# A convolution, FFT-mixer and FFN block on one core: the mixer rewritten as a real DFT with mirror pairs

## The chip, the cores and the metric

One core of a Trainium2 chip runs the whole program. The metric is the device time of one execution in microseconds (us). The kernel before takes 9553.09 us in the three runs given with it (9535.19 to 9569.67). TensorE (PE) does matrix products, VectorE (DVE) and ScalarE (ACT) do elementwise work, GpSimd (POOL) is nearly idle, SyncE (SP) issues the transfers. A trace also records the clock that TensorE was granted: 1.0 is full speed, and here only 1.0 and 0.5 occur, so that a mean of 0.83 means one third of the time at half speed.

## The reference, cut to what matters

Input x is (32, 96, 56, 56) in fp32. Three layers follow one another.

```python
# 1. inverted-residual convolution, 96 -> 576 -> 96 channels, depthwise 3x3 between, + x
# 2. t: 3136 tokens of 96 channels per image
#    h = relu(bn(layer_norm(t) @ w1.T))              # 192 channels
#    X = fft(h, axis=tokens, norm='ortho')
#    xr = relu(X.real * rd - X.imag * id + rb)
#    xi = relu(X.imag * rd + X.real * id + ib)
#    y = ifft(xr + 1j * xi).real                     # along tokens
#    t = t + bn(y @ w2.T)                            # back to 96 channels
# 3. t = t + ffn(layer_norm(t)), operands quantised to fp8, sums to fp16
```

The transform has 3136 = 56 x 56 points and is done in two stages of 56 by matrix products, with twiddle factors between.

## The kernel before

Four streams of small jobs are interleaved by a schedule in units of one image: the convolution (a strip of 14 rows at a time, four strips an image), the projection with the first DFT stage, the spectrum (second stage, rectifier, first inverse stage), and the inverse with the FFN. The generators are "skewed": when a new job enters a stream, every job already in that stream advances by one stage.

The mixer before, with cuts marked:

```python
def project(img, s, g0):                  # tokens doubled: rows 0-55 real, 56-111 imaginary copy
    for q in range(g):                    # g = 4, 4, 4, 2 of the strip's 14 rows
        nc.tensor.matmul(pv[0:SK, q, 0:HA], lhsT=lnx[:, g0 + q, :, :]..., rhs=watt, ...)   # L457
    nc.vector.scalar_tensor_tensor(z, pv, 0.0, ri, ALU.max, ALU.mult)                       # L465
    yield
    for j in range(g // 2):
        nc.tensor.matmul(ps[0:SK, j, 0:2*HA], lhsT=wa, rhs=z[:, 2*j:2*j+2, :], ...)         # L476
    # ... ACT evacuates to ya, transfer to DRAM
def spectrum(img, kg):                    # 14 jobs of 4 columns an image
    # ... load yb
    for q in range(4):
        nc.tensor.matmul(pv[0:SK, q, 0:HA], lhsT=wb[:, 4*kg+q, :], rhs=yb[:, q, :], ...)    # L518
    evacuate(v, pv, relu=True)
    yield
    for j in range(2):
        nc.tensor.matmul(ps[0:SK, j, 0:2*HA], lhsT=wc, rhs=v[:, 2*j:2*j+2, :], ...)         # L526
    # ... evacuate to gc, transfer to DRAM
    inverted[img] = inverted.get(img, 0) + 4
def spectrum_jobs(img):
    for kg in range(S // 4):
        yield lambda: projected.get(img) == S, spectrum(img, kg)
def mix_ffn(img, ng):                     # 8 jobs an image
    nc.sync.dma_start(out=gd, in_=...)
    yield
    ps = psum()
    for q in range(NG):
        for c in range(2):
            nc.tensor.matmul(ps[0:C, c, ...], lhsT=gd[:, q, C*c:C*(c+1)], rhs=wd[:, NG*ng+q, :], ...)  # L550
    evacuate(y, ps)
    yield
    # w2a on y (L562), add to the tokens, layer norm (L245, L257, L274), FFN ...
def ffn_jobs(img):
    for ng in range(S // NG):
        yield lambda: inverted.get(img) == S, mix_ffn(img, ng)     # the gate
    # ... as many empty steps
```

The convolution, which the change does not touch, runs eight of nine taps of 512 channels on DVE, the ninth on ACT, and the remaining 64 channels on PE:

```python
for dr, dc in TAPS:                       # 9
    if (dr, dc) == (0, 0):
        nc.scalar.activation(dst, src, AF.Copy, scale=w)
    else:
        nc.vector.scalar_tensor_tensor(dst, src, w, dst, ALU.mult, ALU.add)    # L386
```

## Time and profile before

| | before |
|---|---|
| span of the profiled run | 9559 us |
| PE busy, mean granted clock | 8315 us, 0.835 |
| DVE busy | 6353 us |
| ACT busy | 3542 us |
| moved by transfers | 712 MB |
| period of one image in the steady state | 288 us |

The period is read from the instruction that finishes a strip's tokens (128 of them): the first starts at 120.1 us, the last at 9266.6 us, so (9266.6 - 120.1) / 127 x 4 = 288 us. Busy shares are unions of intervals; in a row of a group the busy time is followed by the mean duration of one instruction. A matmul's duration is modelled; its cost in a dense stream is the distance from one start to the next. The prediction shows the lines themselves.

### The profile page before, as it was taken

What the parts mean: (1) busy time and instruction counts of PE and PEld (TensorE: products, weight loads), DVE (VectorE), ACT (ScalarE), POOL (GpSimd) and SP (SyncE); (2) the same over time, 40 slices, a digit from 0 to 9 for tenths busy, and PEclk for the clock granted to TensorE, in tenths of its full rate; (3) what the DMA queues carried; (4) which work ended last, traced back from release to release, by engine and by line L of the source; (5) the groups of instructions that cost most, each with busy time, mean ns of one, the idle gap of its engine ahead of it and who ended that gap; (6) DMA issues with size and microseconds to landing.
All of it is one profiled execution on the core that took longest, in us unless ns stands there. A gap on an engine that the chain in (4) does not pass through costs nothing.

```text
span 9559.2 us, 100499 instructions
## 1 busy us (share of the span) xinstructions
PE 8315.1 (87%) x39424; PEld 5424.0 (57%) x39424; DVE 6353.1 (66%) x10129; ACT 3542.0 (37%) x4744; POOL 13.2 (0%) x72
## 2 busy tenths in 40 slices
PE   5888889888898888898888988888988888888888
PEld 2555556555565555555555655555655556555566
DVE  6766676666766667766677666676666776666753
ACT  2333343333433334433334333344333343333432
POOL 0000000000000000000000000000000000000000
PEclk8988798887987888888889878888888888888986
DMA  1222222222222222222222222222222222222222
GB/s 44 67 76 72 77 73 77 71 73 78 77 72 76 70 77 79 68 83 72 73 80 73 77 76 73 75 79 68 80 74 70 82 65 82 72 75 79 76 85 81
DMA packets 582785, 711.58 MB, mean 74 GB/s; under 512 B 35484, under 2 KB 476520, under 8 KB 582088
## 3 DMA queue, kind: packets, MB, share of 16 engines
q1 hardware_dynamic: 582314, 705.17, 25.6%
q8 instruction: 312, 5.11, 0.2%
q14 instruction: 159, 1.30, 0.0%
HBM read 358.22 MB, written 346.82 MB: 74 GB/s over the span
## 4 chain that ended last, share of the span: by engine, by line
PE 64%; DVE 22%; ACT 7%; DMA 3%; issue 3%; SPq 0%; ACTq 0%; DVEq 0%
DVE acc L386 16%; PE ps L550 10%; PE ps L562 6%; PE ps L274 5%; PE ps L358 5%; PE ps L526 5%; PE po L402 5%; PE ps L245 5%; PE ps L335 4%; PE ps L257 4%; PE ps L476 4%; PE ps L518 4%; PE ps L457 3%; ACT acc L389 2%; DVE z L465 2%
## 5 line engine op out<-in xcount | busy, mean ns | idle before, releaser
L386 DVE SCALAR_TENSOR_TENSOR acc<-hs,wdw,acc 128x770 f32<-128x770 f32 (+3 forms) x4096 | 4072.0, 1007 | 124.8 <-ACT acc L384 86.5
L402 PE MATMUL po<-acc,w2T 128*96 128x392 f32 x2048 | 941.0, 573 | 430.7 <-ACT acc L389 430.7
L550 PEld LDWEIGHTS ps<-wd,gd 112*96 112x96 f32 x7168 | 1046.0, 247 | 341.5 <-issue 307.5
L550 PE MATMUL ps<-wd,gd 112*96 112x56 f32 x7168 | 1031.5, 331 | 183.0 <-DMA gd<-gdr 183.0
L235 DVE COPY gc<-ps 112x768 f32<-112x768 f32 x417 | 397.5, 953 | 879.6 <-PE ps L526 879.6
L358 PE MATMUL ps<-xs,w1T 96*128 96x448 f32 x2048 | 861.7, 548 | 8.8 <-ACT ya L480 7.9
L389 ACT ACTIVATE acc<-acc,sbd 128x784 f32<-128x784 f32 x512 | 531.7, 1039 | 720.7 <-DVE acc L386 718.5
L402 PEld LDWEIGHTS po<-acc,w2T 128*96 128x96 f32 x2048 | 355.9, 187 | 779.0 <-ACT acc L389 563.5
L366 ACT ACTIVATE hs<-ps,sb 128x896 f32<-128x896 f32 x512 | 558.6, 1091 | 562.0 <-PE ps L358 561.9
L476 PE MATMUL ps<-z,wa 112*112 112x384 f32 x1792 | 743.2, 535 | 6.2 <-DVE z L465 6.2
L457 PE MATMUL ps<-watt,lnx 97*112 97x192 f32 x3584 | 721.0, 344 | 0.0
L245 PE MATMUL ps<-t,mean_w 96*96 96x392 f32 x1024 | 565.3, 664 | 161.3 <-ACT acc L389 97.0
L457 PEld LDWEIGHTS ps<-watt,lnx 97*112 97x112 f32 x3584 | 629.7, 188 | 132.8 <-issue 35.3
L526 PE MATMUL ps<-v,wc 112*112 112x384 f32 x1792 | 692.5, 510 | 5.7 <-ACT v L231 5.5
L518 PEld LDWEIGHTS ps<-yb,wb 114*112 114x112 f32 x3584 | 594.8, 177 | 180.1 <-issue 54.8
L518 PE MATMUL ps<-yb,wb 114*112 114x192 f32 x3584 | 673.8, 328 | 2.6 <-DMA yb<-ydr 2.6
L480 ACT ACTIVATE ya<-ps 112x768 f32<-112x768 f32 (+1 forms) x512 | 370.6, 724 | 741.2 <-PE ps L476 741.2
L562 PE MATMUL ps<-y,w2a 96*96 96x392 f32 x1024 | 599.0, 728 | 33.8 <-DVE y L235 32.9
L465 DVE SCALAR_TENSOR_TENSOR z<-ps,ri 112x768 f32<-112x768 f32 (+1 forms) x512 | 436.8, 853 | 234.3 <-PE ps L457 231.3
L358 PEld LDWEIGHTS ps<-xs,w1T 96*128 96x128 f32 x2048 | 372.3, 190 | 339.4 <-issue 266.1
L526 PEld LDWEIGHTS ps<-v,wc 112*112 112x112 f32 x1792 | 327.4, 187 | 292.4 <-issue 127.7
L235 DVE COPY y<-ps 96x784 f32<-96x784 f32 x128 | 124.2, 971 | 553.2 <-PE ps L550 553.2
(142 smaller groups left out, 8533.8 us busy)
## 6 DMA issues: line engine op xcount, KB each, us to landing
yb<-ydr SPq DMA_DIRECT2D x448, 336.0 KB, 3.3
gdr<-gc SPq DMA_DIRECT2D x448, 336.0 KB, 3.9
gd<-gdr SPq DMA_DIRECT2D x256, 588.0 KB, 4.4
ydr<-ya SPq DMA_DIRECT2D x384, 336.0 KB, 2.7
xs<-in_x_dram SPq DMA_DIRECT2D x128, 336.0 KB, 3.2
out_dram<-t SPq DMA_DIRECT2D x256, 147.0 KB, 1.9
ydr<-ya SPq DMA_DIRECT2D x128, 168.0 KB
wb<-in_wb_dram SPq DMA_DIRECT2D x1, 2793.0 KB
```

The lines of the kernel that those rows point to most:

```text
L245: nc.tensor.matmul(ps[0:C, j, 0:per], lhsT=mean_w, rhs=t[:, j * per : (j + 1) * per], start=True, stop=True)
L358: nc.tensor.matmul(ps[:, j, 0:448], lhsT=w1T[:, 128 * k : 128 * (k + 1)], rhs=xt[:, 8 * j : 8 * j + 8, :], start=True, stop=True,)
L386: nc.vector.scalar_tensor_tensor(dst, src, w, dst, ALU.mult, ALU.add)
L389: nc.scalar.activation(a2, a2, AF.Relu, bias=sbd[:, 1, k : k + 1], scale=sbd[:, 0, k : k + 1])
L402: nc.tensor.matmul(po[img, s][0:C, j, 0:NB2], lhsT=w2T[:, k, :], rhs=a2[:, NB2 * j : NB2 * (j + 1)], start=False, stop=(k == NK - 1),)
L457: nc.tensor.matmul(pv[0:SK, q, 0:HA], lhsT=lnx[:, g0 + q, :, :].rearrange("p a c -> p (a c)"), rhs=watt, start=True, stop=True,)
L465: nc.vector.scalar_tensor_tensor(z[:, 0:g, :], pv[0:SK, 0:g, 0:HA], 0.0, ri.unsqueeze(1).to_broadcast([SK, g, HA]), ALU.max, ALU.mult,)
L476: nc.tensor.matmul(ps[0:SK, j, 0 : 2 * HA], lhsT=wa, rhs=z[:, 2 * j : 2 * j + 2, :], start=True, stop=True)
L518: nc.tensor.matmul(pv[0:SK, q, 0:HA], lhsT=wb[:, 4 * kg + q, :], rhs=yb[:, q, :], start=True, stop=True)
L526: nc.tensor.matmul(ps[0:SK, j, 0 : 2 * HA], lhsT=wc, rhs=v[:, 2 * j : 2 * j + 2, :], start=True, stop=True)
L550: nc.tensor.matmul(ps[0:C, c, q * S : (q + 1) * S], lhsT=gd[:, q, C * c : C * (c + 1)], rhs=wd[:, NG * ng + q, :], start=True, stop=True,)
L562: nc.tensor.matmul(ps[0:C, 0, 0:NW], lhsT=w2a[:, c, :], rhs=y[:, c, :], start=(c == 0), stop=(c == 1))
```

## The change

The input of the transform is real, so of the 56 first-stage outputs only 29 are independent, and the outputs of the second stage pair up with their mirror images. The change uses this: (1) the first norm is folded into centred weights and a scale per token, so that tokens are no longer doubled; (2) 28 slots replace 56 columns in the spectrum, and the data, not the constants, are the stationary operand; (3) the rectifier works on both members of a mirror pair at once, in ten elementwise instructions instead of one; (4) the second projection w2a stands ahead of the inverse, so that the inverse works on 96 channels instead of 192. The core of the diff:

```diff
-            nc.tensor.matmul(pv[0:SK, q, 0:HA], lhsT=lnx[...], rhs=watt, ...)
+            nc.tensor.matmul(pv[0:SK, q, 0:HA], lhsT=ts[:, SK*k:SK*(k+1)], rhs=watt, ...)   # 7, not 14, a strip
+            nc.vector.scalar_tensor_tensor(z[:, q, :], pv[0:SK, q, 0:HA], fac[...], nsh, ALU.mult, ALU.max)
 ...
-    for q in range(4): matmul(..., lhsT=wb[:, 4*kg+q, :], rhs=yb[:, q, :])
-    evacuate(v, ..., relu=True)
+    for c in range(2):                                    # channel halves
+        for q in range(n): matmul(..., lhsT=yb[:, q, C*c:C*(c+1)], rhs=wb[:, s0+q, :])      # 114 columns
+        nc.scalar.activation(p, a, AF.Identity, bias=rb, scale=r)
+        nc.scalar.activation(m, b, AF.Abs, scale=i)
+        nc.scalar.activation(z[:, :, 0:NF], a, AF.Relu, bias=rb2, scale=r2)
+        nc.vector.tensor_add(m, m, p)
+        nc.vector.tensor_max(z[:, :, 0:NF], z[:, :, 0:NF], m)
+        nc.scalar.activation(u, a, AF.Identity, bias=ib, scale=i)
+        nc.vector.scalar_tensor_tensor(t, b, nr, u, ALU.mult, ALU.add)
+        nc.scalar.activation(t, t, AF.Relu)
+        nc.vector.scalar_tensor_tensor(u, b, r, u, ALU.mult, ALU.add)
+        nc.vector.scalar_tensor_tensor(z[:, :, NF:NF2], u, 0.0, t, ALU.max, ALU.subtract)
+        yield
+    for q in range(n):
+        for c in range(2): matmul(..., lhsT=zs[:, c, q, :], rhs=w2a[:, c, :])                # to frequencies
 ...
 def spectrum_jobs(img):
-    for kg in range(S // 4):
-        yield lambda: projected.get(img) == S, spectrum(img, kg)
+    for s0 in range(0, P2, Q):                            # 4 jobs of 8 slots, each with 3 empty steps
+        yield lambda: projected.get(img) == P2, spectrum(img, s0)
+        for _ in range(3):
+            yield True, iter(())
 ...  # mix_ffn
-    for q in range(NG):
-        for c in range(2): matmul(..., lhsT=gd[:, q, C*c:C*(c+1)], rhs=wd[:, NG*ng+q, :])    # 14, 56 columns
-    evacuate(y, ...); yield; w2a on y
+    for q in range(g): matmul(..., lhsT=gd[:, q, :], rhs=wd[:, t0+q, :])                     # 3 or 4, 112 columns
```

## The prediction

> **What bounds the kernel now.** I read the page's busy shares and slices first, then the timeline of TensorE (to get real matmul rates), then stretches of one image's period, because shares are averages over unlike stages.
>
> The page's header, busy shares and slice rows:
>
> ```profile
> span 9559.2 us, 100499 instructions
> ...
> PE 8315.1 (87%) x39424; PEld 5424.0 (57%) x39424; DVE 6353.1 (66%) x10129; ACT 3542.0 (37%) x4744; POOL 13.2 (0%) x72
> ...
> PE   5888889888898888898888988888988888888888
> ...
> DVE  6766676666766667766677666676666776666753
> ...
> PEclk8988798887987888888889878888888888888986
> DMA  1222222222222222222222222222222222222222
> ```
>
> PE is busy 87% but its granted clock is only 0.7 to 0.9; DMA is at two tenths and cannot be the bound. Matmul durations are modelled, so I take rates from start to start in the PE timeline (start, us, ..., count), in a stretch at full clock:
>
> ```profile
> 3016.74 2.51 PE L550 MATMUL ps<-wd,gd 112*96 112x56 f32 x28
> 3019.09 1.56 PE L274 MATMUL ps<-ident,ra 98*96 98x98 f32 x16
> ...
> 3051.32 0.92 PE L274 MATMUL ps<-ident,rf 98*96 98x98 f32 x8
> 3052.08 0.81 PE L257 MATMUL ps<-mean_w,sqf 96*98 96x1 f32 x8
> ...
> 3055.00 1.45 PE L526 MATMUL ps<-v,wc 112*112 112x384 f32 x4
> 3056.29 1.47 PE L518 MATMUL ps<-yb,wb 114*112 114x192 f32 x8
> 3057.59 0.67 PE L589 MATMUL ps<-h,w2q 128*96 128x392 fp8e5 x3
> ```
>
> 384 columns: 1.29/4 = 322 ns a record; 192 columns: 1.30/8 = 163 ns; 98 columns: 0.76/8 = 95 ns; 56 columns behind 96 weight columns (L550): 2.35/28 = 84 ns. An fp32 matmul of the program leaves two records (L526: 14 groups x 2 x 32 images = 896 matmuls, 1792 records). So wide matmuls cost 0.84 ns a column and record, thin ones never less than their weight load. Applying such rates to all counts gives **about 6790 us of PE work at full clock**, over the page's mean clock 0.835 some 8130 us, 85% of the span: PE is the bound on average.
>
> Stretches of one image (columns: length, then busy us of PE, PEld, DVE, ACT, POOL, then clock, DMA share, GB/s) show that this is a mixture:
>
> ```profile
> 5072.00:5096.00 24.00, 23.80 (x121) 15.84 (x120) 23.21 (x46) 14.50 (x23) 0.00 (x0) 1.00 0.33 95
> ...
> 5192.00:5216.00 24.00, 16.34 (x45) 7.89 (x44) 23.71 (x26) 9.51 (x10) 0.00 (x0) 0.83 0.12 36
> ...
> 5240.00:5264.00 24.00, 17.97 (x76) 11.42 (x75) 12.50 (x13) 7.42 (x10) 0.00 (x0) 0.89 0.60 173
> 5264.00:5288.00 24.00, 22.94 (x94) 16.80 (x94) 5.46 (x12) 1.97 (x4) 0.00 (x0) 0.50 0.27 76
> 5288.00:5312.00 24.00, 23.92 (x120) 18.75 (x120) 7.23 (x24) 4.58 (x8) 0.00 (x0) 0.54 0.19 51
> ...
> 5264.00:5324.00 60.00, 58.85 (x311) 42.02 (x310) 14.89 (x38) 11.35 (x18) 0.00 (x0) 0.62 0.24 63
> 5324.00:5552.00 228.00, 193.68 (x908) 121.96 (x906) 182.71 (x277) 99.19 (x131) 0.30 (x2) 0.91 0.27 79
> ```
>
> The period is 288 us (13.9 strips of tokens end per 1000 us, four make an image). Some 228 us of it are a mixed stage in which DVE is 80% and PE 85% busy, with DVE full at times (23.71 of 24). The other 60 us are a **burst**: the inverse transform of an image is gated on all its spectrum, and at the gate six steps of mix-and-FFN come with no convolution between them. PE first waits 5.2 us for the data just written to DRAM, then runs L550, L562 and the norms at clock 0.50, with DVE idle.
>
> **What the Trainium skill says.** (1) "TensorE: Matmul & The Clock Gate", section on LDWEIGHTS: a load takes columns / 1.2 ns. The trace agrees: 98 columns give 82 ns, and the L257 records (98 weight columns, 1 moving) start (3052.75 - 3052.08)/8 = 84 ns apart, the next row of that timeline starting at 3052.75. (2) The same page, Part 1: the clock halves after an idle window and returns after about 3.4 us of activity. The halving agrees (0.50 after the 5.2 us wait); the return does not: PE is 99% busy for 48 us and stays near 0.50. I read this as thin, load-bound matmuls not counting as activity; that is a guess. (3) "ScalarE: Activation LUTs", section What ACT_TABLE_LOAD costs: 186 ns + 0.833 ns an element, each pointer operand about 93 ns more. Here a PSUM copy of 768 takes 804 ns (the page gives 826), a scaled copy of 784 takes 946 (932). (4) "VectorE: DVE Perf Modes", Why PSUM operands drop a tier: fp32 with a PSUM operand is one element a cycle at most. Agrees: 112x384 takes 555, 112x768 takes 952 ns, so 1.03 ns an element.
>
> **The change part by part.** All sums over 32 images; PE at full clock.
>
> *PE removed* (records x ns): wd L550 7168 x 84 = 602; w2a L562 1024 x 330 = 338; wb L518 and projection L457 3584 x 163 = 584 each; wc L526 and wa L476 1792 x 322 = 577 each; the first norm's three matmul groups (half of L245, the a-parts of L257 and L274) 169 + 168 + 195 = 532. Sum 3794.
>
> *PE added*: thin matmuls (96 to 114 columns, weights as wide) I put at 105 ns, from the 95 ns of the 98/96 shape. Norm 1 as centred product, 7 a strip, 1792 records = 188; forward wb 2 x 28 x 32 x 2 = 3584 records = 376; second projection the same 376; wd 28 x 32 x 2 = 1792 records = 188. Projection without doubled tokens, 1792 x 163 = 292; wa 28 x 192 columns an image at 2 x 0.84 ns = 289; wc on 28 x 96 columns = 144. Sum 1853. **PE falls by 1941, from 6790 to 4850**, 152 us an image; at 0.83 that is 183.
>
> *DVE removed* (summed durations of rows): evacuations v, gc, y (30 + 398 + 124), z 437, lnx 236, cena 123, small norm work 127: 1475. *Added*: z is now 896 ops of 192 with a pointer scalar, 200 + 210 = 410 ns each, 367 us (the L564 row, 392 from PSUM with pointer, is 620 ns, hence 210 fixed); small norm work 127 again; the rectifier, five ops on 8 x 57 = 456 elements: 624, 624, 686, 686, 627 = 3.25 us, on 4 x 57 2.06 us; an image has 6 of the first and 2 of the second, 23.6 us, 755 in all. Sum 1250. Rows overlap by some 7% (their sum is 6.8 ms, the page's busy 6.35), so DVE goes from 6353 to **about 6140, 192 us an image**. The convolution, 4072 in L386 alone, is untouched.
>
> *ACT*: removed v, gc, y, ya, sqa = 947. Added 896 squares of 96 with a sum (260 ns) 233; ya 206; rectifier 722 + 630 + 722 + 722 + 580 = 3.4 us (2.4 for the small block), 803; g and gc 185. Sum 1427. From 3542 to about 4000: not a bound.
>
> *DMA*: per image 112 x 56 x 192 x 4 B four times becomes half of it twice and a quarter twice: less than half. It was hidden; only the wait at the gate remains, and a smaller constant load at the start (10 to 15 us of the 57 us first wait).
>
> *Moved*: DVE is now the larger load in the mixed stage. An image's burst needs about half the matmul work, since L562 and its evacuation are gone and wd has 14 or fewer thin records for each old 28 + 28: six steps of about 11 us at full clock, 22 to 25 at half. So an image takes: DVE outside the burst 192 - 8 = 184 us at 91% saturation (in the stretches above where PE is not full, DVE reached 91 to 99%) = 202; the stall at the gate 8 to 10; the burst 25: **236 us instead of 288**. First strip at 120 becomes 107; tail after the last strip 293 becomes about 185 (it is mixer and FFN of two images at low clock). Total 107 + 31.75 x 236 + 185 = 7785; I shade it to 7700, as the burst might nearly fill with conv work once PE is free.
>
> **Rivals.** *PE sets it still*: if PE, idling more and running thin matmuls, is held at 0.6, its 152 us become 253 an image and the span 8300 or more. For: clock 0.50 in the burst with PE busy. Against: in the mixed stage the same thin norms ran at 0.91 to 1.00. *The rectifier's ping-pong*: ACT and DVE hand t and u back and forth, each in strict order, with one of three PSUM buffers held some 6 us, 8 times an image; if all of it stood on the path, 40 us an image, 8900 us. Against: other streams lie between, and PSUM allocations fall from about 156 to 104 an image. *DVE saturates fully*: 6140/0.93 = 6600, if the gate vanished too. For: 99% in one stretch. Against: the gate's rule is unchanged (the last stage of the last block still waits for the next image's first step).
>
> **Range and chances.** 82% DVE saturation with a 35 us burst gives 31.75 x 269 + 292 = 8830, 96% with 20 us 31.75 x 220 + 292 = 7280. The first needs several losses at once. I take 7200 to 8200. All rivals but extreme ones beat 9553, so a gain over 2% is nearly sure.
>
> **What would show it.** DVE busy 6.0 to 6.3 ms and about 80% of the span; PE work well under it; wb and second projection near 105 ns start to start; ACT near 4.0 ms; one burst an image of 20 to 30 us at clock near 0.5. It would be wrong if the clock in the mixed stage falls below 0.75, if ACT or DVE show long waits on sp, sm, st, su, or if the thin matmuls take 150 ns or more at full clock.

## More of the kernel before

The schedule's entries give the start and the length of a stream in images:

```python
[skewed(every(conv_jobs)),     ..., 0.0,  1.0, 0],
[skewed(project_jobs()),       ..., 0.3,  1.0, 0],
[skewed(every(spectrum_jobs)), ..., 1.45, 0.8, 0],
[skewed(every(ffn_jobs)),      ..., 2.2,  0.9, 0],
```

## The result, and the profile after

The changed kernel takes 7801.02 us (7785.22 to 7816.11, 4 runs), the kernel before 9544.14 in the same rounds: a ratio of 0.8172, 95% interval 0.8143 to 0.8201. Ratios here are the mean time of one kernel's runs over that of the other's of the same rounds, so not quite the ratio of the medians quoted. Executions over 1.5% slower than the fastest of the same kernel are left out of the means.

The page after, header, busy shares and slices:

```profile
span 7814.3 us, 81935 instructions
...
PE 6311.2 (81%) x29442; PEld 3988.3 (51%) x29442; DVE 5984.6 (77%) x10834; ACT 3932.8 (50%) x7245; POOL 9.5 (0%) x70
...
PE   3788888888888878888888888888888888888887
...
DVE  4878778778787787787787877877777877778864
...
PEclk9877887778877788877788787788787888877876
DMA  1111111111111111111111111111111111111111
```

PE lost 2004 us of busy time and DVE 369, ACT gained 391. PE's clock did not rise with the lighter load, it fell from 0.835 to 0.802. A useful sum is span = DVE busy + DVE idle: before 6353 + 3206, after 5985 + 1830. Of the 1745 us between the two profiled spans, 1376 are idle time of DVE and 369 its work. The chain of work that ended last, by engine, before and after, still lies mostly on PE:

```profile
PE 64%; DVE 22%; ACT 7%; DMA 3%; issue 3%; SPq 0%; ACTq 0%; DVEq 0%
```

```profile
PE 60%; DVE 20%; ACT 13%; DMA 3%; issue 2%; SPq 1%; another core or an unknown queue 0%; DVEq 0%; ACTq 0%
```

Groups of the DVE and ACT lists by shape (busy us, mean ns of one, then idle before and who ended it):

```profile
L520 DVE SCALAR_TENSOR_TENSOR z<-ps,ra,nsh 112x192 f32<-112x192 f32 x896 | 355.4, 409 | 152.7 <-PE ps L515 150.6
L596 DVE SCALAR_TENSOR_TENSOR su<-ps,ric,su 96x456 f32<-96x456 f32 x192 | 131.4, 684 | 2.2
L591 DVE TENSOR_TENSOR sm<-sm,sp 96x456 f32<-96x456 f32 x192 | 120.0, 625 | 134.6 <-ACT sm L589 134.6
...
L497 ACT ACTIVATION_READ_ACCUMULATOR sqa<-ps 112x1 f32 x896 | 175.3, 196 | 0.0
```

The new DVE ops cost what was predicted (409, 684 and 625 ns against 410, 686 and 624). The last row was not foreseen: each of the 896 squares with a sum is followed by a second ACT instruction of 196 ns that reads the sum out.

TensorE's timeline around the gate of one image (start, us, group; in brackets idle before it and its cause):

```profile
4095.01 1.56 PE L448 MATMUL po<-acc,w2T 128*96 128x392 f32 x4 [1.51 <-ACT acc L435]
4100.93 1.78 PE L648 MATMUL ps<-wd,gd 112*96 112x112 f32 x8 [4.37 <-DMA gd<-gdr]
...
4106.27 1.91 PE L448 MATMUL po<-acc,w2T 128*96 128x392 f32 x4
...
4124.05 1.73 PE L573 MATMUL ps<-wb,yb 113*96 113x114 f32 x16
4125.71 1.72 PE L350 MATMUL ps<-xs,w1T 96*64 96x448 f32 x4
```

The wait for gd, the spectrum read back from DRAM for the inverse, is still there (4.37 us), and convolution matmuls (L448, L350) now stand between the mix-and-FFN steps. The 16 thin records of L573 take (4125.71 - 4124.05) / 16 = 104 ns each at full clock.

Two views of stretches of the changed kernel, 24 us each around that gate, then one whole period (length, busy us of PE, PEld, DVE, ACT, POOL, clock, DMA share, GB/s):

```profile
4072.00:4096.00 24.00, 19.48 (x57) 11.01 (x56) 23.23 (x35) 12.21 (x28) 0.00 (x0) 0.69 0.17 49
4096.00:4120.00 24.00, 15.64 (x67) 10.79 (x66) 17.44 (x33) 5.75 (x9) 0.14 (x1) 0.73 0.40 94
4120.00:4144.00 24.00, 21.25 (x128) 14.42 (x130) 11.77 (x32) 13.20 (x23) 0.00 (x0) 0.77 0.16 38
...
4108.00:4168.00 60.00, 53.59 (x333) 36.65 (x331) 38.33 (x92) 32.53 (x62) 0.00 (x0) 0.86 0.16 43
4168.00:4342.00 174.00, 137.13 (x583) 83.80 (x583) 145.93 (x244) 89.45 (x163) 0.28 (x2) 0.81 0.15 42
```

A period is 234 us ((7589.2 - 160.3) / 127 x 4), of which DVE is busy 184. Of its 50 us of idle time, 22 lie in the 60 us behind the gate and 28 in the other 174, where it is 84% busy. Just before the gate DVE is nearly full (23.23 of 24) while PE is 19.48 of 24 us busy at clock 0.69. That PE's pauses cost it its clock there is argued; b_warm, below, shows it for one other pause.

The starts and ends: the first strip is finished at 160 us, 40 later than before; after the last strip 225 us are left, against 293 before.

### The profile page after: what moved, and what is told of

The parts are those of the page before. It is cut to its first block, busy times and chain, and to the rows that moved or that the text cites. A ratio compares the mean times of both kernels' runs of the same rounds, so it can differ in the third digit from the quotient of the medians.

```text
span 7814.3 us, 81935 instructions
## 1 busy us (share of the span) xinstructions
PE 6311.2 (81%) x29442; PEld 3988.3 (51%) x29442; DVE 5984.6 (77%) x10834; ACT 3932.8 (50%) x7245; POOL 9.5 (0%) x70
## 4 chain that ended last, share of the span: by engine, by line
PE 60%; DVE 20%; ACT 13%; DMA 3%; issue 2%; SPq 1%; another core or an unknown queue 0%; DVEq 0%; ACTq 0%
DVE acc L432 13%; PE po L448 9%; PE ps L404 6%; PE ps L602 6%; PE ps L381 5%; PE ps L515 4%; PE ps L291 4%; PE ps L320 3%; PE ps L648 3%; PE ps L528 3%; PE ps L487 3%; PE ps L573 3%; PE ps L303 3%; PE ps L350 3%; DMA gd<-gdr 2%
## 5 line engine op out<-in xcount | busy, mean ns | idle before, releaser
L432 DVE SCALAR_TENSOR_TENSOR acc<-hs,wdw,acc 128x770 f32<-128x770 f32 (+2 forms) x4096 | 4035.3, 1005 | 73.9 <-ACT acc L430 51.4
L448 PE MATMUL po<-acc,w2T 128*96 128x392 f32 x2048 | 1073.5, 652 | 412.9 <-ACT acc L435 412.8
L448 PEld LDWEIGHTS po<-acc,w2T 128*96 128x96 f32 x2048 | 412.0, 216 | 907.9 <-ACT acc L435 557.1
L602 PEld LDWEIGHTS ps<-w2a,zs 96*114 96x114 f32 x3584 | 519.0, 235 | 134.1 <-DVE z L520 41.9
L591 DVE TENSOR_TENSOR sm<-sm,sp 96x456 f32<-96x456 f32 (+1 forms) x256 | 144.9, 566 | 543.2 <-ACT sm L589 543.2
L602 PE MATMUL ps<-w2a,zs 96*114 96x96 f32 x3584 | 528.3, 318 | 29.1 <-ACT y L679 17.6
L430 ACT ACTIVATE acc<-hs,wdw 128x784 f32<-128x784 f32 x512 | 485.9, 949 | 10.5
L573 PEld LDWEIGHTS ps<-wb,yb 113*96 113x96 f32 x3584 | 429.4, 181 | 111.0 <-ACT y L679 54.6
L573 PE MATMUL ps<-wb,yb 113*96 113x114 f32 x3584 | 446.5, 281 | 36.7 <-ACT y L679 31.0
L648 PEld LDWEIGHTS ps<-wd,gd 112*96 112x96 f32 x1792 | 292.3, 224 | 304.4 <-issue 243.9
L381 PE MATMUL ps<-hs,diag 64*64 64x385 f32 (+1 forms) x4608 | 424.0, 493 | 1.4 <-ACT hs L361 1.4
L515 PE MATMUL ps<-watt,t 96*112 96x192 f32 x1792 | 421.8, 386 | 0.8 <-ACT ya L532 0.8
L528 PE MATMUL ps<-z,wa 112*112 112x384 f32 (+1 forms) x1024 | 413.3, 526 | 5.7 <-DVE z L520 5.1
```

What stands on the lines that cost most here:

```text
L381: nc.tensor.matmul(pv[:, :, ca:cb], lhsT=diag[o : o + 64, n, o : o + 64], rhs=hs[o : o + 64, q : q + 7, ca + dc : cb + dc], start=(n == 0) ...
L448: nc.tensor.matmul(po[img, s][0:C, j, 0:NB2], lhsT=w2T[:, k, :], rhs=a2[:, NB2 * j : NB2 * (j + 1)], start=False, stop=(k == NK - 1),)
L515: nc.tensor.matmul(pv[0:SK, q, 0:HA], lhsT=ts[:, SK * k : SK * (k + 1)], rhs=watt, start=True, stop=True)
L528: nc.tensor.matmul(ps[0:SK, j // 2, 0 : (e - j) * HA], lhsT=wa, rhs=z[:, j:e, :], start=True, stop=True)
L573: nc.tensor.matmul(pv[0:C, q, 0:NF2], lhsT=yb[:, q, C * c : C * (c + 1)], rhs=wb[:, s0 + q, :], start=True, stop=True,)
L602: nc.tensor.matmul(ps[0:NF2, q // 4, C * (q % 4) : C * (q % 4 + 1)], lhsT=zs[:, c, q, :], rhs=w2a[:, c, :], start=(c == 0), stop=(c == 1),)
```

## The experiments

The theory after the result was: before, the mix-and-FFN burst at the gate and PE's load set the time; after, DVE sets the mixed stage (the part of a period outside the burst) and the gate the rest. Twelve kernels were run, each timed in three rounds against the kernel before and profiled once. The number of stretches at half clock over 40 us, and the sum of all time at half clock, are taken from the clock records of each trace.

| run | median us | ratio to before | DVE busy | DVE idle | half clock, us | stretches > 40 us |
|---|---|---|---|---|---|---|
| before | 9544 | 1 | 6353 | 3206 | 3162 | 32 |
| b_pe2 | 9405 | 0.985 | 6355 | 3059 | 2695 | 21 |
| b_tap (wrong result) | 9207 | 0.962 | 5895 | 3248 | 2735 | 23 |
| b_warm | 8863 | 0.927 | 6349 | 2522 | 1541 | 0 |
| b_gate | 8464 | 0.886 | 6277 | 2188 | 1527 | 1 |
| after | 7801 | 0.817 | 5985 | 1830 | 3091 | 1 |
| a_pe2 | 7877 | 0.825 | 5984 | 1890 | 2587 | 1 |
| a_wd3 | 7808 | 0.820 | 5988 | 1831 | 2341 | 0 |
| a_tap (wrong result) | 7316 | 0.766 | 5515 | 1800 | 2213 | 1 |
| a_gate | 7228 | 0.757 | 5903 | 1306 | 2082 | 1 |
| a_gatesetup | 7204 | 0.758 | 5903 | 1287 | 2047 | 1 |
| a_best | 7218 | 0.759 | 5955 | 1252 | 1819 | 1 |
| a_cen | 7213 | 0.756 | 5802 | 1424 | 2059 | 1 |
| a_norect (wrong result) | 6857 | 0.718 | 5317 | 1538 | 1670 | 0 |

Busy and idle are of the profiled run, whose span differs a little from the median. b_tap's median has one slow run in it, its ratio has not.

### The gate, in both kernels: a_gate and b_gate

The last stage of an image's last spectrum job runs only when the stream advances once more, and that is with the next image's first job, 0.25 of an image later than the FFN is due. One or two empty steps at the end of the image mend it.

```diff
 # a_gate
-            for _ in range(3):
+            for _ in range(3 if s0 + Q < P2 else 4):
                 yield True, iter(())
-        [skewed(every(spectrum_jobs)), 4 * -(-P2 // Q), 1.45, 0.8, 0],
+        [skewed(every(spectrum_jobs)), 4 * -(-P2 // Q) + 1, 1.45, 0.8, 0],
 # b_gate
             yield lambda: projected.get(img) == S, spectrum(img, kg)
+        for _ in range(2):
+            yield True, iter(())
-        [skewed(every(spectrum_jobs)), S // 4, 1.45, 0.8, 0],
+        [skewed(every(spectrum_jobs)), S // 4 + 2, 1.45, 0.8, 0],
```

> Changed kernel, with one empty step more at the end of an image's spectrum jobs, so that the last block's last stage runs at step 2.20 of the schedule and not with the next image's first job at 2.45; no work is added or taken. Theory 'gate': of the 50 us an image in which DVE is idle, some 25 lie around the burst of mix-and-FFN steps that catch up after the late gate; with the gate in time the burst is spread, 15 to 20 us an image are saved, and the time falls from 7800 to 7200 to 7350. Rival 'work': the burst's work only moves into the mixed stage, where PE or DVE is full anyway: within 1.5% of 7800.

> Kernel before, with the same mend (two empty steps after the last spectrum job of an image). Theory 'gate': there the burst takes some 57 us of a 288 us period with DVE idle and PE at clock 0.5; spread among the convolution the same matmuls run at 0.9 or more, so that 20 to 30 us an image are saved: 9540 falls to 8600 to 8900, a third to a half of what the change itself gave. Rival 'work': PE is full in both stages, and within 1.5% of 9540.

a_gate took 7227.9 us (7210.52 to 7232.82), 573 less than the changed kernel; b_gate 8463.78 (8458.87 to 8470.21), 1080 less than the kernel before, more than I expected. Both are correct. The busy shares and the clock of a_gate, then of b_gate:

```profile
PE 5894.4 (82%) x29442; PEld 3697.3 (51%) x29442; DVE 5903.1 (82%) x10834; ACT 3925.1 (54%) x7245; POOL 9.5 (0%) x70
...
PEclk8888888888888888888888888888888888888886
```

```profile
PE 7570.7 (89%) x39424; PEld 4974.2 (59%) x39424; DVE 6276.9 (74%) x10129; ACT 3536.8 (42%) x4744; POOL 12.8 (0%) x72
...
PEclk8888988889999999999999999899999999989897
```

DVE's idle time falls by 524 us in a_gate and by 1018 in b_gate, nearly the whole gain in each. So the late gate was a flaw of both kernels, and it cost the kernel before about twice as much. With the gate mended in both, the change is worth 8464 - 7228 = 1236 us, a ratio of 0.7569 / 0.8862 = 0.854, instead of 1743: some 500 us of the measured gain are the change making a flaw of the schedule cheaper. No run takes the change itself apart, so what each of its four parts is worth stays open.

### Is PE the bound? b_pe2, a_pe2 and a_wd3

Matmuls are repeated; the repetition writes the same values over the first.

```diff
 # a_pe2: projection of the changed kernel
+            for _ in range(2):
                 nc.tensor.matmul(pv[0:SK, q, 0:HA], lhsT=ts[:, SK*k:SK*(k+1)], rhs=watt, ...)
 # b_pe2: as many records in the kernel before
-        for q in range(g):
+        for q in sorted([*range(g), *range(g // 2)]):
 # a_wd3: inverse of the changed kernel, 3584 more thin records
+            for _ in range(3):
                 nc.tensor.matmul(ps[0:C, 0, ...], lhsT=gd[:, q, :], rhs=wd[:, t0 + q, :], ...)
```

> Kernel before with as many projection matmuls doubled as add the same 1792 records of 163 ns, 292 us at full clock, 350 at 0.835. If PE was the bound there, as the prediction says, 250 to 380 us show. If DVE or the waits set it even then, under 150.

> Changed kernel with every projection matmul done twice (the second overwrites the first with the same values): 1792 records of 163 ns, 292 us more on PE at full clock, some 365 at the mean clock 0.80; nothing else. Theory 'DVE and waits': PE is no longer the bound of the mixed stage, less than half of it shows: 40 to 160 us. Rival 'PE still sets it': all of it shows, 300 to 400 us.

> Changed kernel with each inverse matmul (wd) done three times, the last one standing: 3584 more thin records of about 105 ns, 376 us more on PE at full clock, like the 292 us that were added to the projection, but all of it in the mix-and-FFN steps, half of them in the burst at the gate. Theory 'it matters where PE work lies': in the burst nothing hides it and the clock is low, so 200 to 600 us show, against 77 of 292 for the projection. Rival 'PE work is hidden in the changed kernel wherever it lies': under 120 us.

b_pe2 took 9404.69 us (9388.75 to 9441.72): 292 us of PE work more, and 140 us **less** time (1.5%, clear of the noise: ratio 0.9816 to 0.9888). a_pe2 took 7877.41 (7858.37 to 7901.53), 76 more. a_wd3 took 7808.08 (7786.07 to 7820.84), 7 more, or by the ratios to before of their rounds (0.8204 and 0.8172) some 30 more, where I expected 200 to 600; that theory fell.

Why so little shows is not settled, because the clock moved with the work: the time at half clock falls as PE is kept busier (3091, 2587, 2341 us). Half of each fall is what the clock gave back to a busy PE (an estimate): 252 of the 292 us added in a_pe2 and 375 of the 376 added in a_wd3. PE's busy time accordingly rose by only 100 and 74 us (6311, 6411, 6385). So the added work may be hidden behind other engines, or paid by the clock; these runs do not show that PE at its low clock sets nothing in the changed kernel, and the chain above has it at 60%.

In the kernel before, half-clock time fell by 467 us, worth some 234 us by the same estimate, so that of the 292 us added at most about 95 cost time. The clock recovered early in some of the bursts: 21 long half-clock stretches are left of 32. One such burst of b_pe2:

```profile
5216.00:5240.00 24.00, 20.38 (x121) 15.60 (x121) 5.92 (x13) 1.97 (x4) 0.00 (x0) 0.72 0.48 123
5240.00:5264.00 24.00, 23.44 (x207) 16.21 (x206) 7.91 (x25) 8.39 (x12) 0.00 (x0) 1.00 0.28 77
```

Here the clock returns in the middle of the burst, after 13.7 us at half, and the burst runs on at 1.0: its six inverse groups end 36 us after the first began, where the kernel before takes 52 us at 0.50 and 0.54 (72 of the 207 records in the second row are tap matmuls that follow the burst). So "PE is busy 87%, hence the bound" was no safe step for the kernel before: much of that busy time was half-speed time.

### The clock in the burst: b_warm

Twelve wide dummy matmuls stand ahead of the first inverse matmuls of each image, in the wait for gd.

```diff
         ps = psum()
+        if ng == 0:
+            for _ in range(12):
+                nc.tensor.matmul(ps[0:C, 0, 0:NW], lhsT=mean_w, rhs=tok[img, 0][:, 0:NW], ...)
         for q in range(NG):
```

> Kernel before, with 12 wide dummy matmuls (384 to 392 columns, 24 records of 330 ns, 7.9 us at full clock) ahead of the first inverse matmuls of each image; they read the tokens, write columns that the real matmuls overwrite, and need no transfer, so they fill the 5 us in which PE waits for gd. They add 250 us of PE work over 32 images. Theory 'clock': the half clock of 51 to 61 us that the trace of before shows once an image starts from this wait; with PE kept busy the clock stays at 1.0, the burst's PE work of about 25 us at full clock no longer takes 50, and 15 to 25 us an image are saved after the dummies' cost: 9540 falls to 8750 to 9150, and the half-clock stretches over 40 us are gone. Rival 'thin matmuls hold it down': the clock falls to 0.5 within the burst all the same, and the time is 9540 or up to 200 more.

b_warm took 8862.51 us (8837.13 to 8872.52), correct: 7.3% less than before by adding 250 us of useless work. The first inverse group of one image in the kernel before, then the dummies and the first group after them in b_warm, then its stretches:

```profile
5260.35 4.70 PE L550 MATMUL ps<-wd,gd 112*96 112x56 f32 x28 [5.23 <-DMA gd<-gdr]
```

```profile
5178.18 8.06 PE L550 MATMUL ps<-t,mean_w 96*96 96x392 f32 x24
5187.21 2.58 PE L555 MATMUL ps<-wd,gd 112*96 112x56 f32 x28 [0.97 <-DMA gd<-gdr]
```

```profile
5168.00:5192.00 24.00, 23.03 (x100) 13.17 (x99) 11.09 (x12) 6.09 (x8) 0.00 (x0) 1.00 0.57 157
5192.00:5216.00 24.00, 23.43 (x194) 18.48 (x193) 12.14 (x33) 6.55 (x12) 0.00 (x0) 1.00 0.50 135
5216.00:5240.00 24.00, 24.00 (x176) 14.45 (x175) 12.14 (x25) 8.68 (x12) 0.00 (x0) 1.00 0.19 54
```

The wait before the first inverse group is 0.97 us instead of 5.2, the burst stays at 1.0, its 28 inverse records take 2.58 us instead of 4.70, and no half-clock stretch over 40 us is left. So the pause is what lets the clock fall, and the guess in the prediction, that thin matmuls do not count as activity, fails at this point: once the clock is up, the burst keeps it up.

How long it stays down is another matter, and the pause alone does not set it. b_gate has a pause as long at the same place, and the clock is back 10 us later, with convolution matmuls in between:

```profile
5190.91 4.70 PE L552 MATMUL ps<-wd,gd 112*96 112x56 f32 x28 [6.53 <-DMA gd<-gdr]
...
5200.28 2.51 PE L552 MATMUL ps<-wd,gd 112*96 112x56 f32 x28
```

In the kernel before, nothing but the burst's own matmuls follows the pause, and the clock stays down for 41 to 61 us in 30 of the 32 images. In b_pe2 it came back after 13.7 us within such a burst in some images and after 54.6 us in most. What lifts it is open.

### Does DVE set the time? b_tap and a_tap

The ninth tap of 512 channels is left out; the result is wrong (relative error 0.060).

```diff
-        for dr, dc in TAPS:
+        for dr, dc in TAPS[:8]:
             tap = 3 * (dr + 1) + dc + 1
```

> Kernel before without the ninth tap of the depthwise convolution for the first 512 channels (wrong result on purpose): DVE has 512 instructions of 128x715 elements fewer, 490 us, nothing else changes. If PE (with its clock) sets the time of before: under 120 us of it show. Rival, that DVE paces the stretches in which it is 90% full or more: 200 to 350 us show.

> Changed kernel without the ninth tap (wrong result on purpose): 512 DVE instructions of 0.955 us, 486 us, fewer. Theory 'DVE paces the mixed stage, waits the rest': 250 to 450 us of it show, much more than in the kernel before. Rival 'latency': DVE idle grows by what is taken, under 120 show.

a_tap took 7316.43 us (7311.67 to 7322.24), 485 less: as much as the 486 us taken from DVE, a little above my range. b_tap took 9207.39 (9144.35 to 9301.91, one of its runs slow); by its ratio (0.9618, 0.9548 to 0.9687) some 365 less of 490, or 300 to 430. The clock moved in both: half-clock time fell by 878 us in a_tap and by 427 in b_tap, worth at most half of that. In b_tap this leaves at least some 150 us to DVE (an estimate); in a_tap the run does not divide DVE's share from the clock's. DVE's idle time hardly changed there (1830 to 1800), as it would not if DVE set the pace. So DVE's work in the convolution is at least partly on the path in both kernels, where the theory of b_tap had put it at under 120.

### The rectifier: a_norect

```diff
-            # ten instructions of the rectifier
+            nc.scalar.activation(z[:, :, 0:NF], a, AF.Relu, bias=rb2, scale=r2)
+            nc.scalar.activation(z[:, :, NF:NF2], b, AF.Relu, bias=rb2, scale=r2)
```

> Changed kernel with the complex rectifier reduced to two ReLU evacuations on ScalarE (wrong result on purpose): DVE loses all five of its ops, 753 us of summed durations, ScalarE about 435 net; PE unchanged. Theory 'DVE share': 350 to 650 us show, no more than DVE loses. Rival 'ping-pong': the hand-overs between ScalarE and DVE and the PSUM buffer held for them cost beyond the busy time, and over 750 us show.

It took 6857.24 us (6854.69 to 6864.22), wrong (relative error 0.035): 944 less. Busy shares:

```profile
PE 5639.9 (82%) x29442; PEld 3566.7 (52%) x29442; DVE 5316.7 (78%) x9554; ACT 3553.4 (52%) x6477; POOL 9.9 (0%) x70
```

DVE lost 668 us of busy time and ACT 379; 276 us more than DVE's share went. The hand-overs of the rectifier may cost that, as the rival had it: in the changed kernel DVE idles 543 us in all before L591, waiting for ACT's sm. But a shorter ACT queue may have given part of it, and so may the clock, as half-clock time fell from 3091 to 1670 us. The run does not divide the three.

### Towards a better version: a_gatesetup, a_best and a_cen

```diff
 # a_gatesetup = a_gate, and in the setup:
+    load_strip(0, 0); load_strip(0, 1)         # right after w1T
+    # the block that makes watt, sh and the yb rows moved up, behind the load of vec
-    nc.sync.dma_start(out=wb..., in_=d["wb"]);  nc.sync.dma_start(out=wd..., in_=d["wd"])
+    # both moved to the end of the setup
 # a_best = a_gatesetup, and in the tap matmuls of the last 64 channels:
+            if n in (2, 5):
+                yield
 # a_cen = a_gatesetup, and in the norm ahead of the FFN:
-        matmul(..., lhsT=mean_w, ...);  nc.vector.tensor_sub(cv, t, ps);  activation(sq, cen, AF.Square)
+        matmul(..., lhsT=cen_w, ...);   activation(cv, ps, AF.Copy);      activation(sq, ps, AF.Square)
```

> Changed kernel with the gate in time, and with the setup reordered: the first two strips of x and the row for the centred projection weights are loaded first, the two large DFT constants last. In the changed kernel the first convolution matmul starts at 97 us, 40 later than in the kernel before, because its queue of transfers and PE's setup matmul stand ahead of it. Theory: the first strip is ready 60 to 85 us earlier and all of it shows: 7228 falls to 7140 to 7175. Rival: the start is hidden by the stages that follow: within 20 us of 7228.

> As the run with gate and setup, and the tap matmuls of the last 64 channels (36 in a row, 6 us of PE at full clock, twice an image) split over three steps. Theory 'lump': in the trace of the changed kernel DVE waits up to 13 us while this lump stands ahead of the next convolution matmuls; split, 5 to 10 us an image are saved: 160 to 320 us below the run with gate and setup. Rival: the order on PE stays much the same, and the accumulator bank is held longer: within 1%.

> As the run with gate and setup, and the norm ahead of the FFN multiplies by the centring matrix instead of the mean matrix, so that DVE's subtraction (256 instructions, 142 us) goes and ScalarE copies and squares the centred values from PSUM instead (about 135 us more there; PE the same). Theory 'DVE and its chain set the time, ScalarE and PE have room': 7204 falls by 100 to 200, to 7000 to 7100. Rival 'ScalarE's order is as much on the path': within 50 us of 7204 or slower.

a_gatesetup took 7203.74 us (7191.64 to 7214.26), 24 less than a_gate, not 53 to 88; and as it ran in another call, whose runs of before were 20 us faster too, its ratio (0.7575) is no better than that of a_gate (0.7569). The start shows why so little came of it. First rows of PE in the changed kernel, then the row of ACT in a_gatesetup that the convolution waits for:

```profile
81.22 0.95 PE L241 MATMUL ps<-w,cen_w 96*96 96x192 f32 x2 [81.22 <-DVE w L239]
97.25 3.22 PE L350 MATMUL ps<-xs,w1T 96*64 96x448 f32 x4 [15.08 <-DMA xs<-in_x_dram]
```

```profile
79.86 1.29 ACT L363 ACTIVATE hs<-ps,sb 64x448 f32<-64x448 f32 x2 [57.30 <-DMA yb<-sh]
```

In the changed kernel the setup's own matmul (L241) and the loads hold the convolution until 97 us. With the new order its first matmul runs at 19.6 us, but ACT then waits until 79.9 for the 16 small transfers of the row sh into yb. I take this to be the memory of the setup's tiles, which later tiles use again; that is argued, not shown. The first strip is ready at 136 instead of 161 us. Whether these 25 us (0.35%) show in the time, the intervals of the two runs (0.3% each way) do not tell.

a_best took 7218.06 (7209.42 to 7221.6): splitting the lump of tap matmuls gave nothing. a_cen took 7212.71 (7207.57 to 7226.94), its ratio 0.7562 (0.7538 to 0.7586) against 0.7575: DVE lost 101 us of busy time, ACT gained 75, and nothing clear of the noise came of it. So a microsecond of DVE, with the clock that came with it, counts fully in the convolution's taps, and hardly in the norm of the FFN, at least when ACT takes it over. "DVE is the bound" is too coarse: the runs fit a chain of a strip (taps, ACT's ReLU, PE's second convolution) with DVE as its longest member, though none isolates that chain. Which of the other waits hold the remaining 1250 to 1420 us of DVE's idle time stays open.

All four kernels with the gate mended, a_gate, a_gatesetup, a_best and a_cen, beat both kernels, with ratios from 0.7562 to 0.7585 that their intervals do not separate. The simplest of them is a_gate: one empty step, 7228 us, 0.7569 (0.7544 to 0.7594).

## Why the prediction was right or wrong

The time was right: 7801 in a range of 7200 to 8200 around 7700, and the unshaded sum of its steps was 7785. The steps were not all right.

- **Costs of the added work: right.** Thin matmuls 96 to 104 ns for 105 predicted, the z op 409 for 410, the rectifier's DVE ops 625 to 684 for 624 to 686. DVE busy came to 5985 where 6140 was predicted, ACT to 3933 where about 4000 was. ACT's extra read of each sum (175 us) was missed, and other terms were sized a little too high.
- **The period: right as a sum, its parts not.** 236 us were predicted, 234 measured. The prediction had 202 us of mixed stage with DVE 91% busy, 8 to 10 of stall and 25 of burst. The trace has 174 us with DVE 84% busy and 60 us behind the gate in which the convolution runs along at 40% of its rate (its taps keep DVE busy for 15.2 of 60 us, against 110 of 174). The 91% came from chosen stretches; in the row at 5240 PE is not full either and DVE is at 52%. That the two errors cancel is luck.
- **"PE is the bound on average": a step that failed.** b_pe2 added 292 us of PE work and became faster. The step is dividing PE's work by the mean clock and calling the quotient a load: the clock is not given, it went from 0.835 to 0.857 with more work (b_pe2) and to 0.913 with dummies in a pause (b_warm).
- **"The burst at the gate with PE at clock 0.5": right for the kernel before, and larger than thought.** b_gate and b_warm show it with 1080 and some 690 us. Its guess (thin matmuls do not count as activity) was wrong in that they keep the clock up in b_warm; the 5 us pause brings it down, and why it then stays down is open. PE was 98% busy in these 48 us (22.94 + 23.92 of 48), not 99.
- **Its own signs: two did not hold.** The burst of 20 to 30 us near clock 0.5 did not appear: the 60 us behind the gate run at 0.86 with convolution in them, and one half-clock stretch over 40 us is left. And DVE waits 543 us in all on sm, up to 14.7 us at once, which was to count against the prediction. Clock (0.81 in the mixed stage), busy times and matmul costs came as said.
- **Rival "PE sets it still at a low clock": its premise came, its size did not, and the rest is open.** The clock fell to 0.802, not to 0.6, and the time is not 8300. PE work added to the changed kernel shows little (7 of 376 us, 76 of 292; by the ratios of the rounds some 30 and 73), but the clock rose with it.
- **Rival "ping-pong": perhaps partly right.** a_norect gives up to 276 us beyond DVE's busy time; the 40 us an image that the rival put would have been 1280, added to 7785 some 9050 and not the 8900 written.
- **Head and tail: wrong, in the same direction.** The start was predicted 13 us shorter and became 40 longer, because the set-up's matmul for the folded norm (at 81.2 us) and the 16 transfers of sh stand ahead of the load of x, which is issued at 93.3 us; the tail came to 225 us instead of 185. Together they add 53 + 40 = 93 us to the sum of 7785, and the shorter period takes 31.75 x 2 = 64 back; the shading to 7700 had no ground.

## What to carry to other kernels

Before counting a busy TensorE as the bound, look at its granted clock stretch by stretch, and add some work to it, watching the clock too: if the time does not rise, either the work was hidden or the clock paid for it, and in the second case the engine can still be the bound. A gate that waits for the last stage of a software pipeline should be checked for what drives that last stage; here one empty step was worth 7% in the changed kernel and two were worth 11% in the one before. Read the gain of a large change with such flaws mended on both sides, or the flaw's share is credited to the change.

## What the Trainium skill lacked or had wrong

- "TensorE: Matmul & The Clock Gate", Part 1, has the clock return after about 3.4 us of activity. In the kernel before it stays at 0.5 for 41 to 61 us in 30 of 32 images, in the one shown with PE 96% busy or more after a pause of 5.2 us; the same matmuls run at 1.0 when 24 wide records (8.06 us) fill the pause (b_warm). The page's caveats distrust the clock records and tell of one clock stuck for over 50 us, at another ratio; here the matmuls' own starts confirm the half speed (28 records in 4.4 us, 2.35 at full clock).
- The same page gives a back-to-back gap of N / 2.4 + 2.5 ns without the data type. An fp32 matmul here leaves two records of twice that each: 322 ns for 384 columns. "FP8 and Floating Point Precision" does name four passes for true fp32, and these two records at two cycles a column agree with it.
- "ScalarE: Activation LUTs" mentions the accumulator output, but not its price: here each is a second instruction of 196 ns (896 of them, 175 us).
- "TensorE: Matmul & The Clock Gate" also warns of idle gaps between bursts of matmuls; that dummy matmuls put into such a gap more than pay for themselves is on no page that I read: 9549 to 8863 us here with 250 us of them added.
